# Attention scores by one level of Strassen's algorithm, and x in a fixed ring of four buffers

## The chip, the core and the metric

The kernel runs on one core of one Trainium2 chip. The metric is the device time in microseconds (us) from start to end of one execution. The kernel before takes 1821.4 us (median of 3 runs, 1821.21 to 1821.41). The core has a matrix engine (PE, with its weight loads shown apart as PEld), a vector engine (DVE), a scalar engine (ACT), a general engine (POOL, or GpSimd) and queues that issue DMA transfers (SP among others).

## What is computed

Two graph layers over 64 matrices of 256 tokens and 512 features, with one 256x256 adjacency of zeros and ones. Cut to what matters:

```python
def layer0(h, adj, Wq, Wk, Wv):
    q, k, v = h @ Wq.T, h @ Wk.T, h @ Wv.T
    rel = adj.T[None] * (q @ k.transpose(0, 2, 1))        # the scores
    rel = rel / norm(rel, axis=2, keepdims=True)
    return rel @ v

def layer1(h, adj, weight, bias):
    return (adj @ h) @ weight + bias

x = x + layer0(relu(layernorm(x)), adj, Wq, Wk, Wv)
x = x + layer1(relu(layernorm(x)), adj, weight, bias)
```

The kernel folds Wq and Wk into one matrix M beforehand, so that per batch it needs G = M h, scores h G, V = h Wv, the product of scores and V, the gather adj @ h and the mix with weight.

## The kernel before

Batches are worked on in pairs (32 pairs, 512 tokens each). All large products but three are done by one level of Strassen's algorithm in Winograd's form: seven products of half-size blocks in place of eight, with sums of blocks as operands and additions of the results. The projections G and V and the mix are done so; the scores, the product with V (attend) and the gather are plain. The same scheme serves all:

```python
def left_sums(at, tag, i):                # 4 sums of blocks of the activations, on DVE
    s = work.tile([P, 4, HC, HT_], F32, tag=tag)
    a = left_blocks(at)
    nc.vector.tensor_add(s[:, 0], a(1, 0), a(1, 1))
    nc.vector.tensor_sub(s[:, 1], s[:, 0], a(0, 0))
    nc.vector.tensor_sub(s[:, 2], a(0, 0), a(1, 0))
    nc.vector.tensor_sub(s[:, 3], a(0, 1), s[:, 1])

def winograd(product, take):              # take: read a bank of results out
    product(bank_a, 1, True);   take(0, 0, bank_a, True)
    product(bank_c, 5, True);   take(1, 1, bank_c, True)
    product(bank_a, 6, False);  take(0, 1, bank_a, True)
    product(bank_c, 3, False);  take(0, 1, bank_c, False)
    product(bank_a, 7, False);  take(1, 1, bank_a, False)
    product(bank_b, 2, True);   take(0, 0, bank_b, False)
    product(bank_a, 4, False);  take(1, 0, bank_a, True)
```

Each product there is four matmuls with 256 moving columns; a False in product means that it adds to what its bank holds. In a projection, the first take of a block is an ACT copy and a later one a DVE addition. The scores:

```python
def scores(i):
    for b in range(NB):                                   # 2 batches of a pair
        for m in range(NC):
            for e in range(DC):                           # 4 parts of the features
                nc.tensor.matmul(pm[:, m, :], ht[:, e, m, ts(b, P)], g[:, e, :, b, :],
                                 start=(e == 0), stop=(e == DC - 1))   # 256 columns, L300
        nc.vector.tensor_mul(rel[:, b], pm, adj_sb)       # L304
        nc.scalar.activation(sq[:, b], rel[:, b], AF.Square)
    nc.gpsimd.tensor_tensor(sqs, sq[:, :, 0], sq[:, :, 1], ALU.add)
```

The relu of the second layer is split into two parts that the gather multiplies exactly, and then the bias is added on POOL:

```python
def ln1_relu(i, scale_shift, exact):
    for c in range(TC):                                   # 4 chunks of 128x512
        h = whole.tile([P, D], F32, tag="h2c")            # 2 buffers
        relu_chunk(h, src, scale_shift, c)                # ACT
        nc.scalar.copy(dst[:, 0, c, :], h)                # ACT, cast (h2s)
        nc.vector.tensor_sub(dst[:, 1, c, :], h, dst[:, 0, c, :])   # DVE (h2s), L221
    for c in range(TC):
        nc.gpsimd.tensor_tensor(xt[:, c], xt[:, c], bias_bc, ALU.add)   # POOL, L346
```

The order of a pair's stages, in which a scheduler then moves instructions of an engine ahead where it sees fit:

```python
for i in range(NP):
    nxt = i + 1 < NP
    if i + 3 < NP: load(i + 3)
    scores(i)
    if i > 0: gather_sums(i - 1)          # left_sums of the gather's result, ys
    if i > 0 and nxt: mix(i - 1)
    if nxt: transpose_blocks(i + 1)       # 8 DVE transposes, and left_sums, hs
    attend(i)                             # matmuls pu and pn, rn, update of x
    if nxt: project_g(i + 1)
    scale_shift = norm(flat(X[i]))        # DVE statistics
    if nxt: project_v(i + 1)
    elif i > 0: mix(i - 1)
    ln1_relu(i, scale_shift, exact)
    if i + 2 < NP:
        ln0(i + 2)                        # statistics, relu h
        place_blocks(i + 2)               # 16 DMAs
    gather(i, exact)
```

Of the kernel before, what the change touches and what calls it, by code (L numbers as in the profile page):

```python
# [9 lines left out]
F32 = mybir.dt.float32  # L10
F32R = mybir.dt.float32r
I32 = mybir.dt.int32
AF = mybir.ActivationFunctionType
# [5 lines left out]
def kernel(  # L19
# [33 lines left out]
    nc = tc.nc  # L53
    P = 128
    B, N, D = x.shape
    DC = D // P
    NC = N // P
    NB = 2
    TC = NB * NC
    T = NB * N  # L60
    NP = B // NB
    HD = D // 2
    HT_ = T // 2
    HC = DC // 2
    S = 32
# [2 lines left out]
    outs = out.rearrange("(i b) (c p) d -> i p b c d", b=NB, p=P)  # L68

    const = ctx.enter_context(tc.tile_pool(name="const", bufs=1))  # L70
    xpool = ctx.enter_context(tc.tile_pool(name="xpool", bufs=4))
    work = ctx.enter_context(tc.tile_pool(name="work", bufs=1))
    whole = ctx.enter_context(tc.tile_pool(name="whole", bufs=2))
    small = ctx.enter_context(tc.tile_pool(name="small", bufs=3))
    ps_m = ctx.enter_context(tc.tile_pool(name="ps_m", bufs=7, space=bass.MemoryType.PSUM))
    ps_n = ctx.enter_context(tc.tile_pool(name="ps_n", bufs=1, space=bass.MemoryType.PSUM))

    X, H, HP, HT, HS, G, V, R, H2, Y, YS = ({} for _ in range(11))

    def load(i):  # L80
        pool, tag = (const, "x_first") if i == 0 else (xpool, "x")
        X[i] = pool.tile([P, NB, NC, D], F32, tag=tag, name=f"x_{i}")
        nc.sync.dma_start(out=X[i], in_=xs[i])


# [3 lines left out]
    adj_sb = const.tile([P, NC, N], F32, name="adj_sb")  # L89
    w_sb = const.tile([P, DC, D], F32, name="w_sb")  # L90
# [17 lines left out]
        return t.rearrange("p b c d -> p (b c) d")  # L108


    def right_operands(w, name):

        def blk(j, k):
            return w[:, j * HC : (j + 1) * HC, k * HD : (k + 1) * HD]

        t = [const.tile([P, HC, HD], F32, name=f"{name}_t{n}") for n in range(1, 5)]
        nc.vector.tensor_sub(t[0], blk(0, 1), blk(0, 0))
        nc.vector.tensor_sub(t[1], blk(1, 1), t[0])
        nc.vector.tensor_sub(t[2], blk(1, 1), blk(0, 1))
        nc.vector.tensor_sub(t[3], blk(1, 0), t[1])  # L120
        return {1: blk(0, 0), 2: blk(1, 0), 3: blk(1, 1), 4: t[3], 5: t[0], 6: t[1], 7: t[2]}

    def left_blocks(at):

# [11 lines left out]
    def left_operands(at, s):  # L136
        a = left_blocks(at)
        return {1: a(0, 0), 2: a(0, 1), 3: s[:, 3], 4: a(1, 1), 5: s[:, 0], 6: s[:, 1], 7: s[:, 2]}

    def winograd(product, take):  # L140


        bank_a = ps_m.tile([P, 512], F32, tag="pm", name="bank_a")
        bank_c = ps_m.tile([P, 512], F32, tag="pm", name="bank_c")
        bank_b = ps_m.tile([P, 512], F32, tag="pm", name="bank_b")
        product(bank_a, 1, True)
        take(0, 0, bank_a, True)
        product(bank_c, 5, True)
        take(1, 1, bank_c, True)
        product(bank_a, 6, False)  # L150
        take(0, 1, bank_a, True)
        product(bank_c, 3, False)
        take(0, 1, bank_c, False)
        product(bank_a, 7, False)
        take(1, 1, bank_a, False)
        product(bank_b, 2, True)
        take(0, 0, bank_b, False)
        product(bank_a, 4, False)
        take(1, 0, bank_a, True)
# [13 lines left out]
    def product_weights_moving(left, right):  # L173
# [8 lines left out]
                    )  # L182
        return product


    def norm(src):

# [34 lines left out]


    def ln0(i):
        pool, tag = (const, "h_first") if i == 0 else (work, "h")
        H[i] = pool.tile([P, TC, D], F32, tag=tag, name=f"h_{i}")
        relu(H[i], flat(X[i]), norm(flat(X[i])))

    def new_ht(i):
        HT[i] = work.tile([P, DC, NC, NB * P], F32, tag="ht", name=f"ht_{i}")  # L230
        return HT[i]
# [13 lines left out]
    def place_blocks(i):  # L245

        h = H.pop(i)
        HP[i] = work.tile([P, TC, DC, P], F32, tag="hp", name=f"hp_{i}")
        hv = h.rearrange("p c (d e) -> p c d e", e=P)
        for j in range(P // S):  # L250
            for k in range(P // S):
                nc.sync.dma_start(
                    out=HP[i][ts(j, S), :, :, ts(k, S)], in_=hv[ts(k, S), :, :, ts(j, S)]
                )

    def transpose_blocks(i):
        hp, ht = HP.pop(i), new_ht(i)
        for d in range(DC):
            for half in range(NC):
                nc.vector.transpose(  # L260
                    ht[:, d, half].rearrange("p (b n) -> p b n", b=NB),
                    hp.rearrange("p (b h) d n -> p b h d n", b=NB)[:, :, half, d],
                )
        HS[i] = left_sums(ht, "hs", i)

    def project_g(i):
        G[i] = work.tile([P, DC, NC, HT_], F32, tag="g", name=f"g_{i}")

        def take(t, k, bank, first):
            dst = G[i][:, k * HC : (k + 1) * HC, t, :]  # L270
            src = bank.rearrange("p (e t) -> p e t", e=HC)
            if first:
                nc.scalar.copy(dst, src)  # L273
            else:
                nc.vector.tensor_add(dst, src, dst)  # L275

        winograd(product_tokens_moving(left_operands(HT[i], HS[i]), m_right), take)

    def project_v(i):
# [9 lines left out]

        winograd(product_weights_moving(left_operands(HT[i], HS[i]), wv_right), take)  # L290

    def scores(i):
        ht, g = HT.pop(i), G.pop(i).rearrange("p e h (b n) -> p e h b n", b=NB)
        rel = work.tile([P, NB, NC, N], F32, tag="rel", name=f"rel_{i}")
        sq = work.tile([P, NB, NC, N], F32, tag="sq", name=f"sq_{i}")
        for b in range(NB):
            pm = ps_m.tile([P, NC, N], F32, tag="pm", name="prel")
            for m in range(NC):
                for e in range(DC):
                    nc.tensor.matmul(  # L300
                        pm[:, m, :], ht[:, e, m, ts(b, P)], g[:, e, :, b, :],
                        start=(e == 0), stop=(e == DC - 1),
                    )
            nc.vector.tensor_mul(rel[:, b], pm, adj_sb)  # L304
            nc.scalar.activation(sq[:, b], rel[:, b], AF.Square)  # L305
        sqs = work.tile([P, NB, N], F32, tag="sqs", name=f"sqs_{i}")
        nc.gpsimd.tensor_tensor(sqs, sq[:, :, 0], sq[:, :, 1], ALU.add)  # L307
        R[i] = (rel, sqs)
# [28 lines left out]
    def ln1_relu(i, scale_shift, exact):  # L337
        xt = flat(X[i])
        if exact:
            H2[i] = work.tile([P, 2, TC, D], F32R, tag="h2", name=f"h2s_{i}")  # L340
            relu_split(H2[i], xt, scale_shift)
        else:
            H2[i] = work.tile([P, 2, TC, D], F32, tag="h2", name=f"h2_{i}")[:, 0]
            relu(H2[i], xt, scale_shift)
        for c in range(TC):
            nc.gpsimd.tensor_tensor(xt[:, c, :], xt[:, c, :], bias_bc, ALU.add)  # L346
# [25 lines left out]
    def mix(i):  # L372
        xt = X.pop(i)

        def take(t, k, bank, first):
            dst = xt[:, :, t, k * HD : (k + 1) * HD]
            nc.vector.tensor_add(dst, bank.rearrange("p (b e) -> p b e", b=NB), dst)  # L377

        winograd(product_weights_moving(left_operands(Y.pop(i), YS.pop(i)), w_right), take)
        if i + 1 < NP:  # L380
            nc.gpsimd.dma_start(out=outs[i], in_=xt)
        else:
            for t in range(NC):
                nc.sync.dma_start(out=outs[i][:, :, t], in_=xt[:, :, t])
# [24 lines left out]
    m_sb = const.tile([P, DC, D], F32, name="m_sb")  # L409
# [13 lines left out]
            nc.tensor.transpose(pt[:, ts(e, P)], wv_sb[:, e, ts(d, P)], ident)  # L423
        nc.scalar.copy(wvt_sb[:, d, :], pt[:, :D])
    ln0(0)
    m_right = right_operands(m_sb, "m")
    wv_right = right_operands(wvt_sb, "wv")
    w_right = right_operands(w_sb, "w")


    def pairs(exact):
        for j in (1, 2):
            if j < NP:
                load(j)
        transposes_by_matmul(0)
        if NP > 1:
            ln0(1)
            place_blocks(1)
        project_v(0)
        project_g(0)  # L440
        for i in range(NP):
            nxt = i + 1 < NP
            if i + 3 < NP:
                load(i + 3)
            scores(i)
            if i > 0:
                gather_sums(i - 1)
            if i > 0 and nxt:
                mix(i - 1)
            if nxt:  # L450
                transpose_blocks(i + 1)
            attend(i)
            if nxt:
                project_g(i + 1)
            scale_shift = norm(flat(X[i]))
            if nxt:
                project_v(i + 1)
            elif i > 0:
                mix(i - 1)
            ln1_relu(i, scale_shift, exact)  # L460
            if i + 2 < NP:
                ln0(i + 2)
                place_blocks(i + 2)
            gather(i, exact)
        gather_sums(NP - 1)
        mix(NP - 1)
# [35 lines left out]
```

## Time and profile before

| | kernel before |
|---|---|
| time, median of 3 runs | 1821.4 us |
| span of the profiled execution | 1819.1 us |
| clock granted to PE | 0.999 of full speed |
| PE busy | 1790.7 us, 8262 matmul records |
| DVE, ACT, POOL busy | 1003.3, 534.4, 254.5 us |
| score matmuls (prel, L300) | 226.4 us, 1024 records |
| HBM traffic | 39 GB/s over the span |

The profile is of one execution. Its page has busy times by engine, the chain of work that ended last (followed back from the last instruction, at each step to what released it) with its shares by engine and line, and groups of instructions by source line, engine, tile and shape, each with its count, its busy time, the mean length of one and the idle time before it. In a row of the timeline stand the start, the length, the engine, the line, the operation, what it writes and reads, the shape and the count; in brackets the idle time before it and what ended that. A row of the chain has start, length, engine, tile and line. A matmul of FP32 operands shows as two records.

### The profile page before, as it was taken

What the parts mean: (1) busy time and instruction counts of PE and PEld (TensorE: products, weight loads), DVE (VectorE), ACT (ScalarE), POOL (GpSimd) and SP (SyncE); (2) the same over time, 40 slices, a digit from 0 to 9 for tenths busy, and PEclk for the clock granted to TensorE, in tenths of its full rate; (3) what the DMA queues carried; (4) which work ended last, traced back from release to release, by engine and by line L of the source; (5) the groups of instructions that cost most, each with busy time, mean ns of one, the idle gap of its engine ahead of it and who ended that gap; (6) DMA issues with size and microseconds to landing.
All of it is one profiled execution on the core that took longest, in us unless ns stands there. A gap on an engine that the chain in (4) does not pass through costs nothing.

```text
span 1819.1 us, 21280 instructions
## 1 busy us (share of the span) xinstructions
PE 1790.7 (98%) x8262; PEld 1470.8 (81%) x8262; DVE 1003.3 (55%) x1992; ACT 534.4 (29%) x943; POOL 254.5 (14%) x200
## 2 busy tenths in 40 slices
PE   7999999999999999999999999999999999999998
PEld 4788887888888888878888878888788888788886
DVE  4555566545556545665455565456654555654554
ACT  3223332223332133322233321333222333213321
POOL 0101111111111011111011110111110111101111
PEclk9999999999999999999999999999999999999999
DMA  6122221221221222212212212222122122122101
GB/s 223 21 47 47 47 70 49 68 70 24 70 60 57 70 47 47 70 50 68 70 24 70 61 56 70 47 47 70 50 66 70 24 70 62 55 70 47 24 24 49
DMA packets 290239, 105.83 MB, mean 58 GB/s; under 512 B 263120, under 2 KB 263120, under 8 KB 290128
## 3 DMA queue, kind: packets, MB, share of 16 engines
q1 hardware_dynamic: 279904, 68.19, 17.9%
q0 software_dynamic: 8592, 33.03, 4.8%
q10 hardware_dynamic: 1632, 3.15, 0.5%
q8 instruction: 67, 1.10, 0.2%
q14 instruction: 44, 0.36, 0.1%
HBM read 38.27 MB, written 33.55 MB: 39 GB/s over the span
## 4 chain that ended last, share of the span: by engine, by line
PE 66%; DVE 23%; ACT 9%; DMA 1%; issue 1%; DVEq 0%; ACTq 0%
PE bank_a L178 19%; PE prel L300 12%; PE pu L317 12%; DVE st L196 8%; PE py L360 7%; PE bank_c L178 7%; DVE h2s L221 7%; PE bank_b L178 6%; DVE x L331 4%; ACT h2c L206 4%; DVE g L275 2%; ACT h2s L220 2%; ACT v L286 2%; ACT h L206 1%; PE pn L326 1%; PE bank_a L166 1%
## 5 line engine op out<-in xcount | busy, mean ns | idle before, releaser
L346 POOL TENSOR_TENSOR x<-x,bias_bc 128x512 f32<-128x512 f32 x128 | 187.9, 1494 | 526.2 <-ACT h2c L206 512.8
L300 PE MATMUL prel<-g,ht 128*128 128x256 f32 x1024 | 226.4, 379 | 0.7 <-ACT g L273 0.7
L317 PE MATMUL pu<-v,rel 128*128 128x512 f32 x512 | 224.9, 592 | 0.0
L300 PEld LDWEIGHTS prel<-g,ht 128*128 128x128 f32 x1024 | 192.3, 190 | 26.0 <-ACT g L273 1.1
L317 PEld LDWEIGHTS pu<-v,rel 128*128 128x128 f32 x512 | 97.3, 190 | 108.8 <-issue 107.1
L221 DVE TENSOR_TENSOR h2s<-h2c,h2s 128x512 fp32r<-128x512 f32 x128 | 128.4, 1041 | 83.6 <-ACT h2s L220 83.6
L328 ACT ACTIVATE rn<-pn 128x4 f32<-128x4 f32 x32 | 5.5, 173 | 564.1 <-PE pn L326 564.1
L196 DVE BATCH_NORM_STATS2 st<-x 128x6 f32<-128x512 f32 x256 | 167.1, 665 | 7.2 <-DMA x<-in_x_dram 7.2
L377 DVE TENSOR_TENSOR x<-bank_a,x 128x512 f32<-128x512 f32 x128 | 88.4, 691 | 108.1 <-PE bank_a L178 108.1
L307 POOL TENSOR_TENSOR sqs<-sq 128x512 f32<-128x512 f32 x32 | 40.6, 1268 | 699.0 <-issue 594.5
L360 PE MATMUL py<-adjt_r,h2s 128*128 128x256 f32 x1024 | 134.8, 289 | 0.1
L178 PE MATMUL bank_a<-wv_t,hs 128*128 128x256 f32 x512 | 127.0, 391 | 7.4 <-ACT v L286 5.1
L360 PEld LDWEIGHTS py<-adjt_r,h2s 128*128 128x128 f32 x1024 | 127.3, 191 | 2.5 <-DVE h2s L221 0.8
L178 PEld LDWEIGHTS bank_a<-wv_t,hs 128*128 128x128 f32 x512 | 92.5, 190 | 40.9 <-ACT v L286 30.7
L206 ACT ACTIVATE h2c<-x,nb,rs 128x512 f32<-128x512 f32 x128 | 100.7, 810 | 80.8 <-DVE mv L197 53.1
L178 PE MATMUL bank_a<-w_t,ys 128*128 128x256 f32 x512 | 121.1, 379 | 1.2 <-DVE x L377 1.2
L166 PE MATMUL bank_a<-hs,m_t 128*128 128x256 f32 x512 | 121.0, 379 | 0.0
L178 PEld LDWEIGHTS bank_a<-w_t,ys 128*128 128x128 f32 x512 | 97.2, 190 | 14.7 <-DVE x L377 1.6
L166 PEld LDWEIGHTS bank_a<-hs,m_t 128*128 128x128 f32 x512 | 97.3, 190 | 13.2
L304 DVE TENSOR_TENSOR rel<-prel,adj_sb 128x512 f32<-128x512 f32 x64 | 44.2, 691 | 115.3 <-PE prel L300 115.3
L206 ACT ACTIVATE h<-x,nb,rs 128x512 f32<-128x512 f32 x128 | 96.8, 807 | 30.3 <-DVE nb L201 30.3
L305 ACT ACTIVATE sq<-rel 128x512 f32<-128x512 f32 x64 | 40.3, 629 | 206.4 <-DVE rel L304 206.4
(104 smaller groups left out, 2712.4 us busy)
## 6 DMA issues: line engine op xcount, KB each, us to landing
x<-in_x_dram SPq DMA_DIRECT2D x32, 1024.0 KB, 5.5
hp<-h SPq DMA_DIRECT2D x496, 64.0 KB, 2.3
out_dram<-x POOLq DMA_DIRECT2D x31, 1024.0 KB, 4.8
wk_sb<-in_L_gnn_Wk_dram ACTq DMA_DIRECT2D x4, 256.0 KB, 5.5
wq_sb<-in_L_gnn_Wq_dram SPq DMA_DIRECT2D x4, 256.0 KB, 6.5
wv_sb<-in_L_gnn_Wv_dram ACTq DMA_DIRECT2D x1, 1024.0 KB, 11.7
w_sb<-in_L_gnn_weight_dram ACTq DMA_DIRECT2D x1, 1024.0 KB, 15.8
out_dram<-x SPq DMA_DIRECT2D x2, 512.0 KB, 3.4
```

The costliest lines, as they stand in the source:

```text
L166: nc.tensor.matmul(bank[:, e * HT_ : (e + 1) * HT_], right[n][:, d, ts(e, P)], left[n][:, d, :], start=(start and e == 0 and d == 0), stop ...
L178: nc.tensor.matmul(bank[:, b * HD : (b + 1) * HD], left[n][:, d, ts(b, P)], right[n][:, d, :], start=(start and b == 0 and d == 0), stop=( ...
L196: nc.vector.bn_stats(st[:, c, :], src[:, c, :])
L206: nc.scalar.activation(dst, src[:, c, :], AF.Relu, bias=nb[:, c : c + 1], scale=rs[:, c : c + 1])
L221: nc.vector.tensor_sub(dst[:, 1, c, :], h, dst[:, 0, c, :].bitcast(F32))
L300: nc.tensor.matmul(pm[:, m, :], ht[:, e, m, ts(b, P)], g[:, e, :, b, :], start=(e == 0), stop=(e == DC - 1),)
L304: nc.vector.tensor_mul(rel[:, b], pm, adj_sb)
L317: nc.tensor.matmul(pm[:, :D], rel[:, b, m, ts(n, P)], v[:, b * NC + m, :], start=(m == 0), stop=(m == NC - 1),)
L331: nc.vector.scalar_tensor_tensor(xt[:, c, :], pu[c][:, :D], rn[:, c : c + 1], xt[:, c, :], op0=ALU.mult, op1=ALU.add,)
L346: nc.gpsimd.tensor_tensor(xt[:, c, :], xt[:, c, :], bias_bc, ALU.add)
L360: nc.tensor.matmul(pm[:, d, :], left[:, b * NC + m, ts(d0 + d, P)], right, start=(n == 0), stop=(n == len(terms) - 1),)
L377: nc.vector.tensor_add(dst, bank.rearrange("p (b e) -> p b e", b=NB), dst)
```

## The change

The scores become one level of Strassen's algorithm too. Its blocks are halves of the tokens on one side and halves of the features in the sum; within a product the two batches are kept apart, so that a matmul has 128 moving columns instead of 256. The left sums (hs) are those that the projections use already. The right operands are sums of blocks of G, computed on DVE once a pair (score_sums). Its purpose is to multiply less: 7 products instead of 8. To make room in SBUF, x is held in a fixed ring of four buffers instead of one and a pool of four, the first h shares its buffer with the transposition blocks, and the right operands (weights too) overwrite one block in place, so that they need three sums of storage and not four.

```diff
-    xpool = ctx.enter_context(tc.tile_pool(name="xpool", bufs=4))
+    ring = [const.tile([P, NB, NC, D], F32, name=f"x_ring{n}") for n in range(4)]
+    blocks = const.tile([P, TC, DC, P], F32, name="blocks")
     def load(i):
-        pool, tag = (const, "x_first") if i == 0 else (xpool, "x")
-        X[i] = pool.tile([P, NB, NC, D], F32, tag=tag, name=f"x_{i}")
+        X[i] = ring[i % len(ring)]
         nc.sync.dma_start(out=X[i], in_=xs[i])
@@
+    def right_operands(b, t):
+        nc.vector.tensor_sub(t[1], b(1, 1), b(0, 1))
+        nc.vector.tensor_sub(b(0, 1), b(0, 1), b(0, 0))
+        nc.vector.tensor_sub(t[0], b(1, 1), b(0, 1))
+        nc.vector.tensor_sub(t[2], b(1, 0), t[0])
+        return {1: b(0, 0), 2: b(1, 0), 3: b(1, 1), 4: t[2], 5: b(0, 1), 6: t[0], 7: t[1]}
@@
+    def product_of_tokens(left, right):
+        def product(bank, n, start):
+            for b in range(NB):
+                for d in range(HC):
+                    nc.tensor.matmul(
+                        bank[:, ts(b, P)], left[n][:, d, ts(b, P)], right[n][:, d, ts(b, P)],
+                        start=(start and b == 0 and d == 0), stop=(d == HC - 1),
+                        skip_group_check=True,
+                    )
+        return product
@@
+    def score_sums(i):
+        g = G.pop(i)
+        t = work.tile([P, 3, HC, HT_], F32, tag="gt", name=f"gt_{i}")
+        G[i] = right_operands(
+            lambda j, k: g[:, j * HC : (j + 1) * HC, k], [t[:, n] for n in range(3)]
+        )
@@ def scores(i):
-        for b in range(NB):
-            pm = ps_m.tile([P, NC, N], F32, tag="pm", name="prel")
-            (16 matmuls of 256 columns)
-            nc.vector.tensor_mul(rel[:, b], pm, adj_sb)
-            nc.scalar.activation(sq[:, b], rel[:, b], AF.Square)
+        def take(t, k, bank, first):
+            dst = rel[:, :, t, ts(k, P)]
+            src = bank[:, :HT_].rearrange("p (b n) -> p b n", b=NB)
+            if first:
+                nc.scalar.copy(dst, src)
+            else:
+                nc.vector.tensor_add(dst, src, dst)
+        winograd(product_of_tokens(left, right), take)
+        for t in range(NC):
+            nc.vector.tensor_mul(
+                rel[:, :, t], rel[:, :, t], adj_sb[:, t : t + 1, :].to_broadcast([P, NB, N])
+            )
+            nc.scalar.activation(sq[:, :, t], rel[:, :, t], AF.Square)
@@ order of the stages
         project_g(0)
+        score_sums(0)
         for i in range(NP):
-            if i + 3 < NP:
-                load(i + 3)
             scores(i)
             gather_sums(i - 1); mix(i - 1)
+            if i + 3 < NP:
+                load(i + 3)
@@
             ln1_relu(i, scale_shift, exact)
+            if nxt:
+                score_sums(i + 1)
             if i + 2 < NP:
                 ln0(i + 2)
```

(Cut: the diff of the weights' operands, of the blocks buffer, and of names.)

## The prediction

> **What bounds the kernel now.** I read the busy table and the chain's shares first, then the chain in order of time for one pair of batches, then the timeline instruction by instruction where that chain leaves PE. Of the page:
>
> ```profile
> PE 1790.7 (98%) x8262; PEld 1470.8 (81%) x8262; DVE 1003.3 (55%) x1992; ACT 534.4 (29%) x943; POOL 254.5 (14%) x200
> ...
> PE 66%; DVE 23%; ACT 9%; DMA 1%; issue 1%; DVEq 0%; ACTq 0%
> ```
>
> Matmuls lie end to end for 98% of the span, yet the chain that ended last spends 32% of it on DVE and ACT. So PE's work and a chain over DVE and ACT are nearly equally long somewhere. The pairs repeat every 55.55 us (the four bias adds on POOL start at 749.57 in one pair, 805.12 in the next). The chain in order of time, for the pair whose norm matmuls end at 794.21:
>
> ```profile
> 793.41 0.80 PE pn L326 x8
> ...
> 794.72 2.73 DVE x L331 x4
> ...
> 806.28 2.39 DVE h2s L221 x2
> 808.67 0.02 issue
> 808.69 0.81 ACT h2c L206
> 809.51 0.47 ACT v L286
> 809.98 0.53 ACT h2s L220
> 810.50 0.02 issue
> 810.53 1.64 DVE h2s L221 x2
> 812.16 0.10 DVE rs L200
> ...
> 812.48 0.81 ACT h L206
> 813.29 0.48 ACT v L286
> 813.77 0.04 issue
> 813.82 1.99 PE bank_a L178 x8
> ```
>
> It leaves PE after the norm matmuls and comes back 19.6 us later, in the V projection: residual update, statistics, the split of the relu into two halves (h2s), reciprocal, the first relu of the next pair (ACT h), an ACT copy that frees bank_a, then product 7 of the V projection. Product 3 before it begins at 811.86 and lasts 8 x 0.216 = 1.73, so PE is ready at 813.59 and waits 0.23 us. **This chain has no slack: what is added to DVE inside it comes out on PE one for one.** The rest of the pair is PE's own queue.
>
> Inside it two h2s subtractions are slow. DVE and POOL, one instruction each (one timeline query per row):
>
> ```profile
> 806.28 0.69 DVE L221 TENSOR_TENSOR h2s<-h2c,h2s 128x512 fp32r<-128x512 f32 x1 [0.89 <-ACT h2s L220]
> 806.89 1.77 DVE L221 TENSOR_TENSOR h2s<-h2c,h2s 128x512 fp32r<-128x512 f32 x1
> 806.35 1.75 POOL L346 TENSOR_TENSOR x<-x,bias_bc 128x512 f32<-128x512 f32 x1
> 808.07 1.71 POOL L346 TENSOR_TENSOR x<-x,bias_bc 128x512 f32<-128x512 f32 x1
> 809.75 1.27 POOL L346 TENSOR_TENSOR x<-x,bias_bc 128x512 f32<-128x512 f32 x1
> ```
>
> The second subtraction shows 1.77 us instead of 0.69: it ends 0.55 us after POOL's second add (806.35 + 1.75 = 808.10), and POOL's third ends 1.13 us after that subtraction. They take turns.
>
> **What the skill says.** "SBUF — State Buffer", section "SBUF: two separate sides": DVE and GpSimd share a port pair held as an exclusive lock for a whole instruction; a DVE operation with two SBUF inputs takes it. The trace agrees: 0.55 and 1.13 us of work, started only when the other side ends. "TensorE: Matmul & The Clock Gate", "LDWEIGHTS": a load takes columns / 1.2 GHz, 107 ns for 128 columns, and "Back-to-back issue gap" says that spacing is set by both load and matmul. The trace shows a load as 190 ns but the spacing agrees better: seven loads with one-column matmuls in 0.86 us, so (0.86 - 0.19) / 6 = 0.112 us each. "FP8 and Floating Point Precision", "TensorE Precision Notes": true FP32 takes four passes. Here each FP32 matmul shows as two records, and one of 256 columns takes 0.216 us, twice 256 / 2.4 GHz: four passes in effect, in agreement.
>
> **The change part by part.** Scores before: 16 matmuls in the code, 32 records of 256 columns, 6.91 us (prel in the chain of another pair, 6.91 for x32). After: seven products of 4 matmuls, 8 records each, 56 records of 128 columns. Half the columns is 256 x 0.216 / 512 = 0.108 us of streaming, below the 0.112 us that a weight load needs, and the number of loads goes from 32 to 56:
>
> ```profile
> 848.80 0.86 PEld L326 LDWEIGHTS pn<-ones,sqs 128*128 128x128 f32 x7 [0.24 <-issue]
> 819.81 1.27 PEld L360 LDWEIGHTS py<-adjt_r,h2s 128*128 128x128 f32 x10
> 26.75 1.47 PE L423 MATMUL ptw<-ident,wv_sb 128*128 128x128 f32 x12
> ```
>
> These are the load-bound streams of this kernel: 0.112 (first row), (1.27 - 0.19) / 9 = 0.120 for the gather, (1.47 - 0.27) / 11 = 0.109 for the transposes. I choose 0.113, nearest to the FP32 loads of the first row: 56 x 0.113 = 6.33 us. **The 12.5% of multiplications saved becomes 0.58 us a pair (between 0.19 and 0.81), because the loads rose by 75%.**
>
> Score outputs: a copy or an addition per product, 256 columns each, where there were two multiplications from PSUM. A product takes 8 x 0.113 = 0.90 us; bank_a comes back two products later. PE's results reach ACT about 0.2 us after the matmuls (in the timeline of g, a product ends at 853.14 and its copy begins at 853.34) and a half-size copy is an estimate of 0.37 us from the 0.58 of a full one and the 0.17 of the smallest ACT group (rn). 0.57 is below 0.90. DVE has four additions of the same kind at some 0.42, halves of 0.69 with a fixed part, also in time. The two masked multiplications, now from SBUF, end about 1.4 us after the last product, and the mix (12.1 us) lies between them and attend, which reads them. No wait here; the four ys sums stand ahead of these in DVE's order and finish (825.9) before the first addition is due.
>
> Score sums: four DVE subtractions a pair, two SBUF inputs each. The instruction order of the built kernel places them **between the second and the third h2s subtraction**, inside the chain that has no slack, and beside POOL's bias adds. Before, DVE was idle there for 1.87 us (808.66 to 810.53), so without POOL the cost would be 4 x 0.72 - 1.87 = about 1.0 us (0.72 is the distance of dependent sums in the same timeline, as ys at 824.48 and 825.20). With POOL, by turns of 0.55 and 1.13: POOL's third add holds until 809.78; sum 1 to 810.33; POOL's fourth to 811.46; sum 2 to 812.01; then POOL is done, sum 3 to 812.73, sum 4 to 813.45; third h2s to 814.06, fourth to 814.67 (0.61 apart, as the starts at 806.28 and 806.89), against 810.53 + 1.64 = 812.17 before. **The reciprocal, the relu h, the bank_a copy behind it on ACT and product 7 all come 2.50 us later.**
>
> Sum: 2.50 - 0.58 = 1.92 us a pair more. Of 32 pairs 30 have a next relu in this place: 30 x 1.92 = 57.6; the other two gain 0.58 each. 1821.4 + 57.6 - 1.2 = 1877.8, said as 1878.
>
> The x ring: five x buffers become four, but load(i+3) already waits for the output of pair i-1, and lands (848.26 + 5.5) an iteration before its statistics read it. The blocks buffer is one as before. Both cost nothing.
>
> **Rivals.** (A) PE alone sets the end and score sums hide in DVE's 45% idle: then only the 0.58 counts, 32 x 0.58 = 18.6 us less, 1803. For it: 98% PE. Against: the idle share is an average; between 849.60 and 861.70 DVE was busy 10.56 of 12.10 us, and the chain runs through the very place of insertion. (B) The sums fill the 1.87 us gap with little lock contention, +1.0 - 0.58 = +0.4 a pair, 1834. Against: the subtraction of 1.77 us in each pair. (C) Loads do not pipeline at 128 FP32 columns: at 0.130 us a record scores take 7.28, 0.37 more than before, and with the stall 30 x 2.87 = 86, plus 0.7: 1908. For it: the gather's 0.120, above both of its parts. (D) A new wait in the scores, where short products catch up with ACT: each bank wait has only some 0.3 us of slack, so 0.2 us on two of them would add 13 us.
>
> **Range and chances.** The stall could be 1.0 to 2.8, the gain 0.19 to 0.81; the extremes seldom meet. I take 1848 to 1902. Slower by over 2% means above 1857.8, a net of 1.25 us a pair: 0.80. Within 2%: 0.17 (rival B, or a milder lock). Faster by over 2% needs 36.4 us, twice what even rival A gives: 0.03.
>
> **What would show it.** In the profile after: 1792 score records some 0.11 us apart, scores near 6.3 us a pair; four gt/g sums on DVE with a mean well above 0.69, since two of four wait for POOL (1.2 and 1.7 us instead of 0.7); a wait of PE (or its loads) on ACT v of some 2.5 us a pair in the V projection, 75 us or so in total, against 0.23 now; a period near 57.5 us. The prediction is wrong if scores fall well under 6 us, if the sums are not slowed by POOL, or if PE's wait turns up in another stage.

## The result, and the profile after

The changed kernel takes 1895.0 us (median of 4 runs, 1893.9 to 1895.9) against 1821.3: a ratio of 1.0405, 95% interval 1.0387 to 1.0423. The prediction was 1878 us, in a range of 1848 to 1902.

The page of the kernel after, busy times, granted clock and the chain's shares by engine:

```profile
PE 1790.8 (95%) x9030; PEld 1491.0 (79%) x9030; DVE 1176.1 (62%) x2216; ACT 581.7 (31%) x1071; POOL 268.8 (14%) x200
...
PE 63%; DVE 29%; ACT 6%; DMA 1%; issue 1%; ACTq 0%; DVEq 0%
```

PE's busy time is what it was (1790.8 against 1790.7 us), in a span 75.0 us longer, and DVE's share of the chain went from 23% to 29%. Read alone, the busy time would say that Strassen's form saved nothing. It hides two changes that cancel. The scores are shorter by 21 us (0.66 us a pair, below), and products 6 and 7 of the V projection, one group of the page, are longer by 20.3 us. The group before, then after (count, busy time and mean ns of one, idle time before):

```profile
L178 PE MATMUL bank_a<-wv_t,hs 128*128 128x256 f32 x512 | 127.0, 391 | 7.4 <-ACT v L286 5.1
```

```profile
L184 PE MATMUL bank_a<-wv_t,hs 128*128 128x256 f32 x512 | 147.3, 438 | 78.8 <-ACT v L305 75.1
```

The same multiplications last longer because some of them run at half the clock, as shown further down. The 75.1 us of waiting on ACT v are not busy time at all; the chain in order of time shows where they arise. One pair of the kernel after (start, length, engine, tile, line; L239 are the h2s subtractions, L119 to L122 the score sums, L184 the V projection and the mix, L196 the scores):

```profile
840.43 2.37 DVE h2s L239 x2
842.80 1.69 DVE gt L119
844.49 0.02 issue
844.51 1.66 DVE g L120
846.17 0.02 issue
846.19 0.70 DVE gt L121
846.89 0.02 issue
846.92 0.69 DVE gt L122
847.61 1.20 DVE h2s L239 x2
848.81 0.10 DVE rs L218
...
849.13 0.81 ACT h L224
849.94 0.48 ACT v L305
850.42 0.04 issue
850.47 1.99 PE bank_a L184 x8
```

The four sums stand between the second and the third h2s subtraction, and PE's product 7 waits for the end of it all. The first two sums take 1.69 and 1.66 us, the last two 0.70. In the timeline, the first two sums and POOL's third and fourth bias adds of the same pair (one query per row):

```profile
842.72 1.75 DVE L119 TENSOR_TENSOR gt<-g 128x512 f32<-128x512 f32 x1
844.51 1.65 DVE L120 TENSOR_TENSOR g<-g 128x512 f32<-128x512 f32 x1
```

```profile
842.21 1.72 POOL L377 TENSOR_TENSOR x_ring<-x_ring,bias_bc 128x512 f32<-128x512 f32 x1
843.89 1.72 POOL L377 TENSOR_TENSOR x_ring<-x_ring,bias_bc 128x512 f32<-128x512 f32 x1
```

Sum 1 ends at 844.47, 0.54 us after POOL's third add (843.93); POOL's fourth ends at 845.61, 1.14 us after sum 1; sum 2 ends at 846.16, 0.55 us after that. The relu h began 6.20 us after the first h2s subtraction before (806.28 to 812.48), and begins 8.70 us after it now (840.43 to 849.13).

On PE, the timeline of the V projection (products 3 and 7) and two products of the scores:

```profile
846.65 1.24 PE L184 MATMUL bank_c<-wvt_sb,hs 128*128 128x256 f32 x5
850.47 0.70 PE L184 MATMUL bank_a<-wv_t,hs 128*128 128x256 f32 x2 [2.58 <-ACT v L305]
```

```profile
859.58 1.05 PE L196 MATMUL bank_a<-g,ht 128*128 128x128 f32 x8
860.47 1.06 PE L196 MATMUL bank_c<-g,hs 128*128 128x128 f32 x8
861.36 1.06 PE L196 MATMUL bank_a<-gt,hs 128*128 128x128 f32 x8
```

PE idles for 2.58 us in the bracket. Counted as the 0.23 us of before were, from five records of 0.216 us that start at 846.65 and so end at 847.73, the wait until 850.47 is 2.74 us. The products of the scores start 0.893 us apart, so 0.112 us a record and 7 x 0.893 = 6.25 us a pair, against 6.91.

Then there is a thing that the prediction did not have. Of the 28 steady periods (from h2s to h2s, as 840.43, 897.76, 956.50) 15 are 57.34 us long and 13 are 58.7 to 59.0 us. The windows view of the kernel after shows why. Columns: stretch, its length, busy time of PE, PEld, DVE, ACT and POOL with counts, granted clock, share and rate of the DMA:

```profile
787.79:791.20 3.41, 1.35 (x7) 0.84 (x5) 2.49 (x6) 0.82 (x2) 0.00 (x0) 1.00 0.00 0
791.20:794.62 3.42, 2.90 (x7) 2.36 (x8) 0.69 (x1) 2.59 (x4) 0.00 (x0) 0.50 0.01 2
845.82:849.23 3.41, 2.07 (x10) 1.49 (x8) 3.17 (x7) 0.10 (x1) 0.00 (x0) 1.00 0.00 0
849.23:852.65 3.42, 2.18 (x10) 1.95 (x11) 0.84 (x2) 3.31 (x5) 0.00 (x0) 1.00 0.00 0
```

The clock halves for exactly 3.41 us after a stretch in which PE worked only 1.35 of 3.41 us. In the next pair the same wait falls across two such stretches, PE works 2.07 and 2.18 us in them, and the clock stays whole. There are 13 half-clock stretches after such waits (and one at the start); before had none until its last matmul.

### The profile page after: what moved, and what is told of

The parts are those of the page before. It is cut to its first block, busy times and chain, and to the rows that moved or that the text cites. A ratio compares the mean times of both kernels' runs of the same rounds, so it can differ in the third digit from the quotient of the medians.

```text
span 1894.1 us, 23082 instructions
## 1 busy us (share of the span) xinstructions
PE 1790.8 (95%) x9030; PEld 1491.0 (79%) x9030; DVE 1176.1 (62%) x2216; ACT 581.7 (31%) x1071; POOL 268.8 (14%) x200
## 4 chain that ended last, share of the span: by engine, by line
PE 63%; DVE 29%; ACT 6%; DMA 1%; issue 1%; ACTq 0%; DVEq 0%
PE bank_a L184 19%; PE pu L348 12%; DVE st L214 7%; PE py L391 6%; PE bank_c L184 6%; PE bank_a L196 6%; PE bank_b L184 6%; DVE h2s L239 6%; DVE x_ring L362 4%; PE bank_c L196 3%; DVE gt L119 3%; DVE g L120 3%; ACT h2c L224 2%; DVE g L294 2%; PE bank_b L196 2%; PE pn L357 1%
## 5 line engine op out<-in xcount | busy, mean ns | idle before, releaser
L377 POOL TENSOR_TENSOR x_ring<-x_ring,bias_bc 128x512 f32<-128x512 f32 x128 | 202.4, 1609 | 522.6 <-ACT h2c L224 509.2
L184 PE MATMUL bank_a<-wv_t,hs 128*128 128x256 f32 x512 | 147.3, 438 | 78.8 <-ACT v L305 75.1
L184 PEld LDWEIGHTS bank_a<-wv_t,hs 128*128 128x128 f32 x512 | 106.5, 218 | 118.0 <-ACT v L305 102.5
L214 DVE BATCH_NORM_STATS2 st<-x_ring 128x6 f32<-128x512 f32 x256 | 167.2, 666 | 6.1 <-DMA x_ring<-in_x_dram 6.1
L408 DVE TENSOR_TENSOR x_ring<-bank_a,x_ring 128x512 f32<-128x512 f32 x128 | 88.4, 691 | 115.7 <-PE bank_a L184 115.7
L239 DVE TENSOR_TENSOR h2s<-h2c,h2s 128x512 fp32r<-128x512 f32 x128 | 118.6, 967 | 26.2 <-ACT h2s L238 26.2
L224 ACT ACTIVATE h2c<-x_ring,nb,rs 128x512 f32<-128x512 f32 x128 | 100.6, 810 | 79.3 <-DVE nb L219 55.7
L224 ACT ACTIVATE h<-x_ring,nb,rs 128x512 f32<-128x512 f32 x124 | 93.9, 807 | 101.2 <-DVE nb L219 101.2
L184 PE MATMUL bank_c<-wvt_sb,hs 128*128 128x256 f32 x512 | 122.1, 382 | 2.4 <-DVE hs L136 2.4
L184 PE MATMUL bank_a<-w_t,ys 128*128 128x256 f32 x512 | 121.1, 379 | 1.2 <-DVE x_ring L408 1.2
L172 PE MATMUL bank_c<-hs,m_sb 128*128 128x256 f32 x512 | 121.0, 379 | 0.0
L184 PE MATMUL bank_c<-w_sb,ys 128*128 128x256 f32 x512 | 121.0, 379 | 0.0
L184 PEld LDWEIGHTS bank_c<-wvt_sb,hs 128*128 128x128 f32 x512 | 97.8, 191 | 16.1 <-issue 2.7
L138 DVE TENSOR_TENSOR ys<-yt 128x512 f32<-128x512 f32 x32 | 22.2, 693 | 141.2 <-ACT yt L395 141.2
L184 PEld LDWEIGHTS bank_a<-w_t,ys 128*128 128x128 f32 x512 | 97.2, 190 | 14.8 <-DVE x_ring L408 1.6
```

The lines of the kernel that those rows point to most:

```text
L172: nc.tensor.matmul(bank[:, e * HT_ : (e + 1) * HT_], right[n][:, d, ts(e, P)], left[n][:, d, :], start=(start and e == 0 and d == 0), stop ...
L184: nc.tensor.matmul(bank[:, b * HD : (b + 1) * HD], left[n][:, d, ts(b, P)], right[n][:, d, :], start=(start and b == 0 and d == 0), stop=( ...
L214: nc.vector.bn_stats(st[:, c, :], src[:, c, :])
L224: nc.scalar.activation(dst, src[:, c, :], AF.Relu, bias=nb[:, c : c + 1], scale=rs[:, c : c + 1])
L239: nc.vector.tensor_sub(dst[:, 1, c, :], h, dst[:, 0, c, :].bitcast(F32))
```

## The experiments

All this fits, but it is read from one trace. The theory: the sums stand in a chain without slack, they take turns with POOL, PE's idle time follows, and the clock falls because of the idle time. Rivals: the 128-column matmuls themselves are slow or bring the clock down; the place of the sums costs the time whatever POOL does; the ring of x buffers costs something. All ratios below are to the kernel before on the same chip, with their 95% interval.

**Sums out of the chain.** Nothing is left out; only DVE's order changes.

```diff
+                with tc.issue_after(last_shift[0].ins):   # the shift of ln0(i + 2)
+                    score_sums(i + 1)
```

> The changed kernel with the four score sums queued on DVE behind the shift of the next pair's norm, that is out of the chain that releases bank_a in the V projection; nothing is left out. Theory (the sums lengthen that chain by 2.5 us a pair, and PE's idle time there halves its clock in about every second pair): PE's wait on ACT v falls back to about 0.2 us a pair, no half-clock stretch is left, and the shorter scores (6.25 us a pair in place of 6.91) are all that remains, a period of 54.9 us and about 1800 us in all, 0.95 of the changed kernel. Rival (the 128-column matmuls themselves lower the clock or make PE wait): the half-clock stretches stay and the time stays above 1850 us.

Measured: 1802.8 us, ratio 0.9902 (0.9885 to 0.9918); period 54.84 us; clock 0.999 and no half-clock stretch. The four sums take 0.69 us each. The same multiplications in the same shapes, with four DVE instructions moved, are 92 us faster than the changed kernel: the 128-column matmuls neither wait nor lower the clock.

**Sums alone.** The other part of the change by itself: plain scores, and the sums in their place, read by nothing.

```diff
-        winograd(product_of_tokens(left, right), take)
+        (the 16 matmuls of before, and the mask from PSUM)
```

> The changed kernel with the plain scores of before (32 records of 256 columns); the four score sums are still computed in their place, into a buffer that nothing reads. Theory: the sums alone bring the stall and the half clock; period 55.55 + 2.5 = 58.05 us, some 1821 + 30 x 2.5 = 1897, and with half-clock stretches of about 20 us in total 1917 us. Rival (the slow part is the Strassen scores and not the sums): about 1821 to 1830 us.

Measured: 1909.1 us, ratio 1.0489 (1.0471 to 1.0506). The period at full clock is 58.06 us, as expected, so the sums alone bring the wait. The half-clock stretches after such waits are 8 and not some 13, and the longer periods add 13.0 us in place of the 20 that were expected, which is most of what is missing from 1917. The period of 58.06 us is 17.01 times 3.413, so the wait drifts slowly through the stretches: in seven pairs in a row the share of the stretch in which PE has no record rises from 0.525 to 0.576, by about 0.008 a pair, and only after the last of them does the clock fall.

**Filler on PE.** Does the clock fall from idleness? Ten more records are put where PE idles.

```diff
         product(bank_c, 3, False)
+        if fill: fill()          # 5 FP32 matmuls, 256 columns, into a bank nothing reads
         take(0, 1, bank_c, False)
```

> The changed kernel with five more FP32 matmuls of 256 columns (ten records, 2.16 us) in PE's queue between products 3 and 7 of each V projection from the second pair on, into a bank that nothing reads: work added where PE idles for 2.7 us. Theory (the clock is halved because PE idles there): no half-clock stretch is left, every period is 57.34 us, and the time falls by 19 to 22 us to about 1874 us although PE does 65 us more. Rival (the clock falls for power or for the many weight loads): the half-clock stretches stay or grow, and the time stays at 1894 us or above.

Measured: 1878.5, 1878.7 and 1880.8 us, ratio 1.0322 (1.0302 to 1.0343); a fourth execution took 5957.3 us at full clock, for a reason that no trace shows, and is left out. Two rows of its timeline, the filler and product 7:

```profile
839.62 1.89 PE L314 MATMUL fill<-ht,wvt_sb 128*128 128x256 f32 x8
841.94 1.99 PE L186 MATMUL bank_a<-wv_t,hs 128*128 128x256 f32 x8 [0.42 <-ACT v L307]
```

The wait is 0.42 us, every steady period is 57.34 us, and no half-clock stretch is left before the last matmul. PE does 310 more records (67 us) and the kernel is about 16 us faster. It missed the 1874 by about 5 us, of which 4.3 are the filler's own time in the first and the last V projection, where PE did not wait for this chain (periods of 56.66 against 54.51 and 46.85 against 44.67). So it is idle time that brings the clock down here, not load.

**Without POOL's bias adds.** The bias is missing from the output; DVE's order is that of the changed kernel.

```diff
-        for c in range(TC):
-            nc.gpsimd.tensor_tensor(xt[:, c, :], xt[:, c, :], bias_bc, ALU.add)
```

> The changed kernel with POOL's four bias adds a pair left out (the bias is missing from the output); the order of DVE's instructions is the same. Theory (DVE's sums and h2s subtractions take turns with POOL on a shared port): all four sums take 0.7 us, no h2s subtraction is above 0.75 us, PE's wait in the V projection falls below 0.5 us a pair, the period to about 54.5 us, and the time to about 1790 us. Rival (the place of the sums in DVE's order costs the time, whatever POOL does): the sums still delay the chain by 2.8 less 1.9 us of idle time, PE waits more than 1 us a pair and the time is about 1830 us or more.

Measured: 1783.5 us, ratio 0.9797 (0.9781 to 0.9814); period 54.24 us. Its groups by line (count, busy time and mean ns of one, idle time before):

```profile
L239 DVE TENSOR_TENSOR h2s<-h2c,h2s 128x512 fp32r<-128x512 f32 x128 | 82.7, 686 | 26.7 <-ACT h2s L238 26.7
...
L120 DVE TENSOR_TENSOR g<-g 128x512 f32<-128x512 f32 x32 | 22.1, 692 | 1.1
...
L119 DVE TENSOR_TENSOR gt<-g 128x512 f32<-128x512 f32 x32 | 21.9, 684 | 1.7 <-ACT g L292 1.7
```

and the same groups of the changed kernel:

```profile
L239 DVE TENSOR_TENSOR h2s<-h2c,h2s 128x512 fp32r<-128x512 f32 x128 | 118.6, 967 | 26.2 <-ACT h2s L238 26.2
...
L119 DVE TENSOR_TENSOR gt<-g 128x512 f32<-128x512 f32 x32 | 54.1, 1690 | 1.7 <-ACT g L292 1.7
L120 DVE TENSOR_TENSOR g<-g 128x512 f32<-128x512 f32 x32 | 49.9, 1559 | 1.1
```

The sums and the h2s subtractions all take 0.69 us once POOL's bias adds are gone. The place alone does not cost the time. It costs it together with POOL's adds beside it: without them the h2s subtractions are shorter too, and that makes room in the chain for the sums.

**Bias adds held back.** The same without leaving anything out: POOL reads one column of the next norm's shift first.

```diff
+        g = nc.gpsimd.tensor_tensor(gate, nb[:, :1], nb[:, :1], ALU.add)
+        with tc.issue_after(g.ins):
+            (the four bias adds)
```

> The changed kernel, complete, with POOL's four bias adds a pair held back: a one-column add on POOL reads the shift of the next pair's norm first, so that they run after the chain on DVE and not beside it. The sums stay between the second and third h2s subtraction. Theory (turns with POOL on a shared port): as with the bias left out, sums and h2s subtractions at 0.7 us, a period of about 54.2 us and about 1784 us. Rival (leaving POOL's work out helped for another reason, such as the output being ready sooner): no gain or a new wait where the adds now run, 1800 us or more.

Measured: 1784.6 us, ratio 0.9797 (0.9780 to 0.9813), the ratio of the run without bias adds. It is the moment of POOL's work that costs, not the work.

**Both moves.** The sums behind the shift, and POOL held back by a column of the sums' operand.

```diff
+                with tc.issue_after(last_shift[0].ins):
+                    score_sums(i + 1)
+            add_bias(i, G[i + 1][4][:, 0, :1])        # the gate reads a result of the sums
```

> The changed kernel, complete, with the sums behind the shift of the next pair's norm and POOL's bias adds behind the sums. If PE's wait in the V projection is already gone with the bias adds moved alone, nothing is left to win there: 1780 to 1786 us, the same period of 54.2 us. If a wait of 0.2 us a pair is left, 6 us less than with the bias adds moved alone.

Measured: 1780.1 us, ratio 0.9773 (0.9757 to 0.9790), the fastest version, complete. The period is 54.11 us, 0.13 below the one before: a small wait had been left (PE's loads wait 7.7 us in all on ACT v with the bias adds moved alone, and not at all here). Its page has the chain at

```profile
PE 97%; DVE 1%; DMA 1%; ACT 0%; issue 0%; ACTq 0%; DVEq 0%
```

which is what a kernel bound by PE looks like. The busy share hardly tells it: 98% in the kernel before, whose chain was 66% PE, and 99% here.

**The kernel before with its bias adds held back.** The same gate on the shift.

```diff
+            add_bias(i, last_shift[1][:, :1])          # last_shift[1] is nb of ln0(i + 2)
```

> The kernel before, complete, with POOL's bias adds held back in the same way. Theory (the h2s subtractions wait for POOL there too, and PE's two waits of 0.35 and 0.23 us a pair come from that): the waits vanish, a period of 55.0 us in place of 55.55, and about 1804 us. Rival (the kernel before had no such loss): 1821 us.

Measured: 1798.5 us, ratio 0.9873 (0.9857 to 0.9890); period 54.76 us. The gain is 0.79 us a pair and not 0.58, because each of the two products of eight records that waited also lasted 0.10 us longer (1.99 us in the timeline of before, the others 1.89). This is the fair base for the change: 1780.1 against 1798.5, 1.0% less, 0.65 us a pair, which is the 0.66 us that the scores became shorter.

**The ring alone.** Plain scores, no sums, the four x buffers, the shared blocks and the weights' operands in place.

```diff
-            score_sums(i + 1)
-        winograd(product_of_tokens(left, right), take)
+        (the scores of before)
```

> The changed kernel with the plain scores of before and without the score sums: what is left of the change is the ring of four x buffers, the shared blocks buffer and the operands in place. Every theory so far: 1821 us, within 0.3%. If the loads of x or the transposition blocks cost something, it shows as a longer period than 55.55 us.

Measured: 1822.6 us, ratio 1.0008 (0.9999 to 1.0017), period 55.55 to 55.57 us. The ring costs nothing.

**Half the columns.** Do weight loads set the pace of the scores? The fastest version, with every score matmul cut in two of 64 columns.

```diff
-    bank[:, ts(b, P)], left[n][:, d, ts(b, P)], right[n][:, d, ts(b, P)],
+    bank[:, ts(2*b+k, P//2)], left[n][:, d, ts(b, P)], right[n][:, d, ts(2*b+k, P//2)],   # k in 0, 1
```

> The best version so far (changed kernel, complete, sums and bias adds moved out of the chain) with each score matmul cut in two of 64 moving columns: the same multiplications in 112 records in place of 56, each with its own weight load. If weight loads set the spacing, a record keeps about 0.112 us, scores take 12.5 us a pair in place of 6.25, and the time rises by 32 x 6.25 = 200 us to about 1980 us. If streaming sets it, a record of 64 columns takes about 0.056 us and the time stays near 1780 us.

Measured: 1979.0 us, ratio 1.0866 (1.0848 to 1.0884). Two products in its chain in order of time:

```profile
835.84 1.79 PE bank_c L197 x16
837.63 1.79 PE bank_a L197 x16
```

1.79 / 16 = 0.112 us a record, with 64 columns as with 128. How many columns move, up to 128, makes no difference; a record costs 0.112 us. That this cost is the weight load fits the 0.112 us of the one-column norm matmuls, but each record has its own load in every run, so no run tells the load from another fixed cost of a record.

## Why the prediction was right, and what it missed

- **What bounds the kernel.** Right: the chain over DVE and ACT had no slack. A delay of 2.50 us in it came out as a wait of 2.74 us where 0.23 had been, 2.51 more, and moving the sums or POOL's adds took it away.
- **Turns with POOL.** Right, step by step: sum 1, POOL's fourth add and sum 2 end 0.54, 1.14 and 0.55 us after one another, where 0.55 and 1.13 were used. The runs without the bias adds and with them held back show the cause. One estimate beside it was wrong: the sums in this place without POOL were put at about 1.0 us. With the bias adds held back in both kernels they cost 0.14 us (54.24 against 54.76 - 0.66), because the estimate left the h2s subtractions as slow as POOL had made them.
- **Scores.** The mechanism was right: records count and not columns, as the run with half the columns shows; that it is their weight loads is likely and not shown. The size was 6.33 us with the chosen 0.113; measured 6.25, a gain of 0.66 in place of 0.58.
- **Copies, additions, masks.** No wait in the scores; a half-size copy took 0.372 us and an addition 0.424, estimated at 0.37 and 0.42.
- **The net of a pair.** 57.34 - 55.55 = 1.79 us, predicted 1.92.
- **The ring.** Costs nothing, as said.
- **The sum.** 1878 against 1895. The step that failed is that a wait of PE costs its own length and nothing more: the term that was missing is the clock. The 13 longer periods exceed 57.34 us by 1.4 to 1.7 us each, 19.4 us together. With it the account closes: 28 steady periods x 1.79 = 50.1, the clock 19.4, the first and last steady pairs 1.4 and 1.8, and 2.3 before them (with one half-clock stretch in the set-up), 75.0 us in all, the difference of the spans. Without the clock and the set-up the pairs added 53.3 us, 3 less than the 56.4 predicted; those two added 21.7. The list of what would show the prediction wrong had no line for the clock, and none of the rivals contained it. The range was made for other doubts: that it held this term was luck.
- **Rival A** (sums hidden in idle DVE time, 1803 us) is what the kernel does once four instructions are reordered: 1802.8 us. It failed on the place of the sums beside POOL's adds, not on DVE's load.

## What to carry to other kernels

Work added to an engine with idle time is free only outside the chain that has no slack: follow the chain in order of time through the place where the scheduler puts it, and look at which engine takes turns with it at that moment. The busy time of the matrix engine can stay the same while two changes cancel in it. For the FP32 matmuls of this kernel, fewer than 128 moving columns saved nothing; count records, not multiplications. A regular wait of the matrix engine can cost more than its length: here 2.6 us of it brought the clock down in 13 of 28 pairs, for 1.4 to 1.7 us more each.

## What the runs showed of the hardware

- The clock of the matrix engine fell to half for one stretch of 3.413 us after a wait of about 2.6 us. I cut the spans into stretches of 3.413 us in step with the recorded clock changes and counted the share without a PE record in each, apart from the start and the end. In the kernel after, the 13 stretches with the highest share, 0.590 to 0.759, were followed by a half-clock stretch; the next highest, 0.584, was not. In the run with the sums alone, the 8 stretches of 0.576 and above were followed by one, and none of 0.573 and below. So the same wait halved the clock or not by its position in a fixed grid. The share orders the stretches within a trace, but no one limit fits both (0.584 without, 0.576 with), and in the set-ups it fails: 0.517 was followed by a half-clock stretch with the ring alone, 0.582 was not with both moves. The rule therefore rests on the steady pairs of two traces, in which the ends of matmuls are modelled. That idleness is the cause, the filler shows.
- An FP32 record with 64 or 128 moving columns took 0.112 us, and one of 256 columns 0.216 us: at 128 columns and below something other than the columns sets the distance, most likely the weight load.
- A one-column add on POOL that only waits was enough to move 5.9 us of POOL's work out of DVE's way, and brought 23 us to the kernel before.
